# mLSTM: the running sum of the forget gates as a product with a triangle, the sums of the rows one below the other, and gatings first among the streams that are due

## The chip, the cores and the metric

The kernel runs on one core of a Trainium2 chip. A core has a matrix engine (TensorE, PE in the profile; its weight loads are listed apart, as PEld), VectorE (DVE), ScalarE (ACT), GpSimd (POOL) and SyncE (SP), which here only issues DMAs. Each engine works through its own instructions in the order in which the program has them. SBUF is the working memory with 128 partitions; products land in PSUM, which has eight banks of 128 partitions x 512 float32. The metric is the time of one execution on the device, in microseconds; less is better.

## The reference

The input is x of 4 sequences, 512 positions and 256 channels, in float32. Two layers follow. In each, x is normalised, and the outputs of an attention block and of a feed-forward block are added to it.

Layer 0 has an mLSTM block and, beside it, a feed-forward block with eight low-rank experts of which each token uses two. The mLSTM block (8 heads, 16 channels of q and k, 32 of v) computes, for each sequence and head:

```python
logfg = log_sigmoid(f_pre);  Fcum = cumsum(logfg)              # over positions
Dmat  = Fcum[s] - Fcum[t] + i_pre[t],  -inf where t > s
m     = max over t of Dmat;  Smat = exp(Dmat - m)
C     = (q @ k.T / sqrt(dqk)) * Smat
n     = maximum(abs(sum over t of C), exp(-m))
h     = (C / n) @ v
```

followed by a norm of each head, an output gate, w_out, and a gated MLP of 1024 channels (w_gate, w_up, w_down). With g[t] = i_pre[t] - Fcum[t], the row maximum is m[s] = Fcum[s] + max of g[t] over t <= s. So a running sum of logfg and a running maximum of g give all that the exponentials need.

The expert block computes silu(gate) * up for the base and once more for each of two chosen experts, with gate and up shifted by low-rank products. Layer 1 has an attention over the 4 sequences at each position (16 heads) and a feed-forward block of 1024 channels that keeps the two largest of each four.

## The kernel before

Positions are worked off in NJ = 4 tiles j of 128 positions; a tile holds these positions of all B = 4 sequences, so 512 tokens. All products are in float32. TensorE runs a matmul in two passes and a transpose in one, which is why the profile has 3782 of its instructions.

**Order.** The program's order is made by a planner when the kernel is built. Each piece of work is a Python generator, a stream, that yields the time from which it can go on; `Clock` (from line 51) keeps a modelled time for each engine and tile, and `Flow` (from line 223) picks the next stream. `flow.run(main)` steps the main stream whenever it is due and no other stream is; among the other streams `Flow.next` (line 268) takes the one whose time comes first, streams with a flag last. What a stream issues goes into the queues of all engines in that order, so an instruction on VectorE that waits holds up all that the planner put behind it.

In layer 0 the main stream goes through the experts of a tile (`experts`) and then the MLP of the tile before (`mlp`). Beside it run `routing` (low-rank inputs `low`, by way of the transposes `spread`), `following` (norm, transposes and values `vp` of the next tile), and `attention_of_all`, which runs `mlstm(j)` tile by tile. Layer 1 follows with streams of its own.

**Experts.** `order` (line 1106) lists eleven chunks of up to 128 hidden channels x 256 tokens: one "pair" (two halves of 64 rows, packed into the array at once) and ten whole ones. `base(i)` opens a PSUM bank `chunk` and does the base products (chunk<-xnT,wguT: four matmuls, for the pair eight of 64 rows). `gated` (line 1128) reads the bank: a tanh on ScalarE into `sl`, and, as a stream of its own named `rest`, two operations on VectorE, sl<-sl,chunk and the product into `hid` (base) or into `he` (experts; `he_pair` for the pair, `tmp` for the others). Then the low-rank products of the first and of the second expert are added to the same bank (chunk<-low,lora, steps 1 and 2), each only after the gating before it has read the bank. `acc` collects the products from `he`, and at the end those of `hid` with WdT and of `dw` with BdT. A bank that the gatings still read blocks the next step on TensorE. Four banks are opened in advance only while `low` isn't there; after that the loop opens one per round.

**mLSTM.** `mlstm(j)` takes the gate inputs `gz` (tokens on partitions). The log of the forget gate is worked out on VectorE in about 14 small operations (fz, fp, fa) into `lg`, with the input gate beside it. Two transposes `r_ps` bring both to rows: 32 rows (head x sequence) of 128 positions. On VectorE a scan with multiply and add gives the running sum `f_row`, a subtraction `g_row`, a scan with max the running maximum `m_row`, an addition `fm_row`; `m_end` is the last maximum on a diagonal. `carry` hands the last columns to the next tile. `m_row` goes to DRAM and comes back in two DMAs as `ct`, spread over all partitions. Three transposes and a product with `ones` bring g_row, fm_row, m_row and m_end back to columns in the bank `t_ps`; `cols` copies them to SBUF, and `dec` holds the exponents (four sets of 32 columns), which ScalarE exponentiates. GpSimd scales the values with them (`wv`), TensorE makes the new state from that (`kt_ps`, `st_ps`, in the stream `pass_on`).

Then GpSimd masks `ct`, VectorE subtracts g, ScalarE exponentiates, `qk` (packed, 32 rows at a time) is multiplied in, and `by_columns` (line 869) forms hv = ct x va and the row sums: for each half s of the heads, 16 matmuls of 32 output rows x 128 columns into the bank `sums`, with the sequence b as the column block. `to_tokens` (line 876) transposes the two hv and the sums back to tokens (`tok`, four 128x128 transposes each). After that come `den`, `ss` (GpSimd takes its power -1/2), the output gate (`o_ps`), the transposes `pt`, the product `yp` with w_out, which VectorE adds to `xn`, statistics, and the transposes for the MLP.

**Where rows and columns of this meet in the PE array.** A product with fewer than 128 rows or columns of weights is placed in a part of the array: 64 columns for the pair, 32 columns for hv, sums and st_ps, 32 rows for qk, h_ps and t_ps.

Of the kernel before, what the change touches and what calls it, by code (L numbers as in the profile page):

```python
# [28 lines left out]
BANKS = 8  # L29


@with_exitstack
def layers_kernel(ctx: ExitStack, tc: tile.TileContext, io: dict, out: bass.AP):
# [189 lines left out]
    class Flow:  # L223
# [10 lines left out]
        def add(self, gen, wait=0.0, after=False):  # L234

            self.streams.append([self.now + wait, gen, after])
# [150 lines left out]
    ones = new(const, [B * H, P], "ones")  # L387
    nc.gpsimd.memset(ones, 1.0)
    mhalf = new(const, [P, B * H], "mhalf")
# [17 lines left out]
    for base, step in ((0, -2 * DQK), (2 * DQK - 1, 2 * DQK)):  # L407
        nc.gpsimd.affine_select(
            out=own_pair, in_=own_pair, pattern=[[step, H // 2]], compare_op=ALU.is_ge,
            fill=0.0, base=base, channel_multiplier=1 if step < 0 else -1)  # L410
    def inv_sqrt(o, i):
# [60 lines left out]
    with ExitStack() as l0:  # L472
# [22 lines left out]
        pool.memset(ones_at, 0.0)  # L495
# [152 lines left out]
        def mlstm(j):  # L648
# [23 lines left out]
            for s in range(2):  # L672
# [9 lines left out]
            lg = new(sm, [P, 2, H, B], "lg")  # L682
            lf = lg[:, 0, :, :].rearrange("p h b -> p b h")
            dve.tensor_scalar_mul(
                lg[:, 1, :, :].rearrange("p h b -> p b h"), gz[:, :, 0:H], CAP)
# [12 lines left out]
            dve.scalar_tensor_tensor(lf, fp, -2.0, fa, ALU.mult, ALU.add)  # L698
# [15 lines left out]
            yield from flow.wait(lg, banks=1)  # L714

            r_ps = mm_ps("r_ps")
            for n in range(2):
                transpose(  # L720
                    r_ps[0:HB, n * P : (n + 1) * P], lg[:, n, :, :].rearrange("p h b -> p (h b)"),
                    ident)
            yield from flow.wait(r_ps)
            f_row = new(sm, [HB, P], "f_row", 2)
            dve.tensor_tensor_scan(
                f_row, ones[:, 0:1].to_broadcast([HB, P]), r_ps[0:HB, 0:P],
                0.0 if first else carry["F"], ALU.mult, ALU.add)
            g_row = new(sm, [HB, P], "g_row")
            dve.tensor_tensor(g_row, r_ps[0:HB, P : 2 * P], f_row, ALU.subtract)
            m_row = new(sm, [HB, P], "m_row", 2)  # L730
            dve.tensor_tensor_scan(
                m_row, g_row, g_row, LOWEST if first else carry["M"], ALU.max, ALU.max)
            fm_row = new(sm, [HB, P], "fm_row")
            dve.tensor_tensor(fm_row, f_row, m_row, ALU.add)
            carry["F"], carry["M"] = f_row[:, P - 1 : P], m_row[:, P - 1 : P]
# [811 lines left out]
```

## Time and profile before

| | us |
|---|---|
| median of 3 runs | 775.93 (774.78 to 776.19) |
| the profiled execution | 776.43 |
| its span, first to last instruction | 774.6 |
| TensorE busy | 763.0 (99% of the span), 3782 instructions |
| VectorE busy | 471.4 (61%), 1070 |
| ScalarE busy | 225.7 (29%), 457 |
| GpSimd busy | 160.6 (21%), 151 |
| granted TensorE clock, mean | 1.000 |

A line of a group reads: line, engine, operation, out<-in by tile names, rows*columns of the weights, moved size, count | busy time, mean duration in ns | idle time before it. Nearly all lines say L216, the helper that records every operation; the tile names tell them apart. A line of the timeline has start and duration in us; equal instructions that follow each other are merged, with their count. Products overlap, so the time from one start to the next is shorter than a duration. A line of the waits reads: who waits <- who releases it: us in total, times, longest.

Layer 0 ends near 545 us. The four tiles' mLSTM transposes `r_ps` begin at 28.9, 138.5, 253.9 and 387.2 us.

### The profile page before, as it was taken

The page shows a single profiled execution, that of the slowest core. Times are in us where ns is not written, and L with a number is a line of the kernel's source. Part 1 is how long each engine was busy: PE and PEld are TensorE (multiplying, and loading weights), DVE is VectorE, ACT ScalarE, POOL GpSimd, SP SyncE. Part 2 cuts the span into 40 slices and gives each one's busy share as a digit, 9 for nine tenths or more (in the row PEclk, how much of TensorE's full clock was granted, in tenths as well). Part 3 has the DMA queues.
Part 4 walks back from the last instruction along what each step waited for, and adds up shares of the span by engine and source line. Part 5 has one row for each costly group of instructions (what it writes and reads, how often), then busy time and mean ns, then how long its engine had stood idle before and what let it go on. Part 6 is the DMA issues. An engine that isn't in the chain of part 4 may idle for free.

```text
span 774.6 us, 9712 instructions
## 1 busy us (share of the span) xinstructions
PE 763.0 (99%) x3782; PEld 516.6 (67%) x3782; DVE 471.4 (61%) x1070; ACT 225.7 (29%) x457; POOL 160.6 (21%) x151
## 2 busy tenths in 40 slices
PE   6999999999999999999999999999999999999998
PEld 3677786766657776765777774747545575754487
DVE  4878647977552878634378534332366984837980
ACT  2334314332212342313134312010344305243310
POOL 5322051321230410140030041000333203333000
PEclk9999999999999999999999999999999999999999
DMA  8830000300000300000030120001000000000000
GB/s 253 282 97 1 1 1 1 110 1 1 1 1 1 110 0 1 2 0 1 1 110 1 56 96 14 1 0 55 0 1 0 0 28 1 0 28 0 0 28 29
DMA packets 18975, 25.44 MB, mean 33 GB/s; under 512 B 2800, under 2 KB 12784, under 8 KB 18928
## 3 DMA queue, kind: packets, MB, share of 16 engines
q1 hardware_dynamic: 17408, 24.39, 9.9%
q8 instruction: 30, 0.49, 0.3%
q10 hardware_dynamic: 1520, 0.43, 0.2%
q14 instruction: 17, 0.14, 0.1%
HBM read 22.65 MB, written 2.16 MB: 32 GB/s over the span
## 4 chain that ended last, share of the span: by engine, by line
PE 98%; DVE 1%; DMA 1%; ACT 0%; issue 0%
PE chunk L216 20%; PE yp L216 18%; PE up L216 14%; PE gp L216 14%; PE acc L216 11%; PE qk_ps L216 4%; PE vp L216 2%; PE pt L216 2%; PE v_ps L216 2%; PE o_ps L216 2%; PE lp L216 2%; PE qk L216 1%; PE hv L216 1%; PE sums L216 1%; PE k_ps L216 1%; PE q_ps L216 1%
## 5 line engine op out<-in xcount | busy, mean ns | idle before, releaser
L216 ACT ACTIVATE sl<-chunk 128x256 f32<-128x256 f32 x132 | 50.6, 384 | 134.5 <-PE chunk L216 118.1
L216 PE MATMUL chunk<-low,lora 128*128 128x256 f32 (+1 forms) x384 | 87.3, 385 | 0.9 <-DVE he_pair L216 0.7
L216 PE MATMUL chunk<-xnT,wguT 128*128 128x256 f32 (+1 forms) x384 | 84.5, 384 | 0.0
L216 PEld LDWEIGHTS chunk<-xnT,wguT 128*128 128x128 f32 (+1 forms) x384 | 63.6, 181 | 23.5 <-issue 11.5
L216 PEld LDWEIGHTS chunk<-low,lora 128*128 128x128 f32 (+1 forms) x384 | 63.0, 181 | 14.9 <-issue 2.1
L216 DVE SCALAR_TENSOR_TENSOR sl<-sl,chunk 128x256 f32<-128x256 f32 x132 | 54.4, 412 | 11.3 <-ACT sl L216 10.7
L216 PE MATMUL gp<-xnT,wguT 128*128 128x512 f32 x128 | 60.2, 592 | 0.0
L216 PE MATMUL up<-featT,w_up 128*128 128x512 f32 x128 | 60.2, 592 | 0.0
L216 PE MATMUL gp<-featT,w_gate 128*128 128x512 f32 x128 | 60.1, 592 | 0.0
L216 PE MATMUL up<-xnT,lora 128*128 128x512 f32 x128 | 60.1, 592 | 0.0
L216 PE MATMUL yp<-w_down,hid 128*128 128x256 f32 x256 | 56.2, 379 | 0.0
L216 PE MATMUL yp<-w_gate,hs 128*128 128x256 f32 x256 | 56.2, 379 | 0.0
L216 PEld LDWEIGHTS yp<-w_down,hid 128*128 128x128 f32 x256 | 48.5, 190 | 8.2 <-issue 1.7
L216 PEld LDWEIGHTS yp<-w_gate,hs 128*128 128x128 f32 x256 | 48.6, 190 | 6.6
L216 DVE SCALAR_TENSOR_TENSOR tmp<-tmp,gp 128x512 f32<-128x512 f32 x32 | 21.9, 685 | 42.8 <-ACT tmp L216 42.8
L216 ACT ACTIVATE tmp<-gp 128x512 f32<-128x512 f32 x32 | 19.1, 597 | 96.7 <-PE gp L216 96.7
L216 PEld LDWEIGHTS up<-xnT,lora 128*128 128x128 f32 x128 | 24.3, 190 | 29.3 <-issue 28.0
L216 PEld LDWEIGHTS up<-featT,w_up 128*128 128x128 f32 x128 | 24.1, 190 | 27.9 <-issue 26.3
L216 PEld LDWEIGHTS gp<-xnT,wguT 128*128 128x128 f32 x128 | 24.0, 190 | 27.8 <-issue 27.0
L216 PEld LDWEIGHTS gp<-featT,w_gate 128*128 128x128 f32 x128 | 24.1, 190 | 27.6 <-issue 27.3
L216 POOL TENSOR_TENSOR pd<-k,q 128x256 f32<-128x256 f32 (+3 forms) x16 | 25.3, 1583 | 81.8 <-ACT k L216 81.8
L216 PE MATMUL acc<-WdT,hid 128*128 128x256 f32 (+1 forms) x192 | 40.9, 386 | 0.0
(211 smaller groups left out, 1192.0 us busy)
## 6 DMA issues: line engine op xcount, KB each, us to landing
ct<-m_dram SPq DMA_DIRECT2D x8, 1024.0 KB, 8.1
x<-in_x SPq DMA_DIRECT2D x3, 512.0 KB, 9.6
out<-x SPq DMA_DIRECT2D x6, 256.0 KB, 2.1
w_gate<-in_w_gate SPq DMA_DIRECT2D x1, 1024.0 KB, 6.7
w_up<-in_w_up SPq DMA_DIRECT2D x1, 1024.0 KB, 7.6
w_down<-in_w_down SPq DMA_DIRECT2D x1, 1024.0 KB, 10.6
wguT<-in_f_gate SPq DMA_DIRECT2D x1, 1024.0 KB, 5.0
lora<-in_f_up SPq DMA_DIRECT2D x1, 1024.0 KB, 5.0
```

The source lines that it names most:

```text
L216: return tc.keep_in_program_order(f(*args, **kw))
```

## The change

Five things change, all in layer 0 (the flags are renamed in layer 1 as well).

1. The running sum of the forget gates is no scan: f_ps = triangle x log_f on TensorE, with the new constant `up_to` (ones where the column isn't before the row), while positions are still on partitions. VectorE takes g and f from it into the two halves of `by_pos`, and one 128x128 transpose `r_ps` makes rows of both. The sum starts at zero in each tile; `m_end`, `f_end` and `ends` carry the offset from tile to tile.
2. One scan is left, a max of r_ps with the constant `lowest`, into rows 0 to 31 of `by_row`, which is zero elsewhere. One 128x128 transpose and one product with 64 columns (`at_end`: the last maximum on a diagonal, and log_f, whose column sums are the last running sums) make `t_ps`. `cols` is gone: the operations that made `dec` read `t_ps` in PSUM.
3. The sums of the four sequences go to the same 128 columns of `sums`, in rows 2b + s of each block of 32, so the matmuls of all b accumulate; the copy shrinks to 128 columns and the third `tok` to one transpose.
4. `add(..., after=True)` becomes `turn=1`, and the stream `rest` of `gated` gets `turn=-1`: it goes ahead of every other stream that is due.
5. Where the last opened chunk's base gating isn't done by the planner's clock and a bank is free, the loop in `experts` opens further bases, up to AHEAD = 4 in advance.

On GpSimd the constants and zeroed tiles add a memset of `lowest`, the selection for `up_to` and three memsets to the set-up ahead of the first norm.

```diff
+AHEAD = 4
...
-        def add(self, gen, wait=0.0, after=False):
+        def add(self, gen, wait=0.0, turn=0):
-            self.streams.append([self.now + wait, gen, after])
+            self.streams.append([self.now + wait, gen, turn])
...
-    ones = new(const, [B * H, P], "ones")
+    ones = new(const, [P, P], "ones")
+    lowest = new(const, [B * H, 1], "lowest")
+    nc.gpsimd.memset(lowest, LOWEST)
+    up_to = new(const, [P, P], "up_to")
+    nc.gpsimd.affine_select(
+        out=up_to, in_=ones, pattern=[[1, P]], compare_op=ALU.is_ge, fill=0.0, base=0,
+        channel_multiplier=-1)
...
+        by_pos = new(sm, [P, P], "by_pos")
+        by_row = new(sm, [P, P], "by_row")
+        at_end = new(sm, [P, 2 * HB], "at_end")
+        for t in (ones_at, by_pos, by_row, at_end):
+            pool.memset(t, 0.0)
+        g_col, f_col, log_f = (t.rearrange("p (h b) -> p h b", b=B) for t in (
+            by_pos[:, 0:HB], by_pos[:, HB : 2 * HB], at_end[:, HB:]))
...
-            lg = new(sm, [P, 2, H, B], "lg")
-            dve.tensor_scalar_mul(
-                lg[:, 1, :, :].rearrange("p h b -> p b h"), gz[:, :, 0:H], CAP)
...
+            f_ps = mm_ps("f_ps")
+            mm(f_ps[:, 0:HB], up_to, at_end[:, HB:], start=True, stop=True)
+            f_hb = f_ps[:, 0:HB].rearrange("p (h b) -> p h b", b=B)
+            dve.scalar_tensor_tensor(
+                g_col, gz[:, :, 0:H].rearrange("p b h -> p h b"), CAP, f_hb, ALU.mult,
+                ALU.subtract)
+            dve.tensor_copy(f_col, f_hb)
+            yield from flow.wait(by_pos, banks=1)
             r_ps = mm_ps("r_ps")
-            for n in range(2):
-                transpose(r_ps[0:HB, n * P : (n + 1) * P], lg[:, n, :, :]..., ident)
+            transpose(r_ps[:, 0:P], by_pos, ident)
             yield from flow.wait(r_ps)
-            dve.tensor_tensor_scan(f_row, ones[:, 0:1]..., r_ps[0:HB, 0:P], ..., ALU.mult, ALU.add)
-            dve.tensor_tensor(g_row, r_ps[0:HB, P : 2 * P], f_row, ALU.subtract)
-            dve.tensor_tensor_scan(m_row, g_row, g_row, ..., ALU.max, ALU.max)
-            dve.tensor_tensor(fm_row, f_row, m_row, ALU.add)
+            m_row = by_row[0:HB, :]
+            dve.tensor_tensor_scan(
+                m_row, lowest.to_broadcast([HB, P]), r_ps[0:HB, 0:P],
+                LOWEST if first else carry["M"], ALU.max, ALU.max)
             if not last:
-                dve.tensor_scalar_mul(m_end, ident[0:HB, 0:HB], carry["M"])
+                dve.tensor_scalar_mul(
+                    at_end[0:HB, 0:HB], ident[0:HB, 0:HB], m_row[:, P - 1 : P])
+                dve.tensor_copy(f_end, r_ps[HB : 2 * HB, P - 1 : P])
+                dve.tensor_tensor(m_end, f_end, m_row[:, P - 1 : P], ALU.add)
+                carry["M"] = m_end
...
-            for n, row in enumerate((g_row, fm_row, m_row)):
-                transpose(t_ps[:, n * HB : (n + 1) * HB], row, ident[0:HB, 0:HB])
+            transpose(t_ps[:, 0:P], by_row, ident)
             if not last:
-                mm(t_ps[:, 3 * HB : 4 * HB], ones, m_end, start=True, stop=True)
+                mm(t_ps[:, P : P + 2 * HB], ones, at_end, start=True, stop=True)
             yield from flow.wait(t_ps)
-            dve.tensor_copy(cols..., t_ps...)
-            dve.tensor_scalar_mul(dec[:, 0, :, :], cols[:, 1, :, :], -1.0)
+            m_col = t_ps[:, 0:HB].rearrange("p (h b) -> p h b", b=B)
+            dve.scalar_tensor_tensor(dec[:, 0, :, :], m_col, -1.0, f_col, ALU.mult, ALU.subtract)
...
+                dve.tensor_copy(ends[:, 0, :, :], m_all)
+                dve.tensor_tensor(ends[:, 1, :, :], f_all, m_all, ALU.add)
...
-                        mm(out[32 * r : 32 * r + 32, cols_of(b)], lhsT(b, r),
-                           ct[s][:, r, cols_of(b)], start=start and b == 0, stop=stop, ...)
+                        o = out[32 * r : 32 * r + 32, :]
+                        mm(o if n_of(o) == P else o[:, cols_of(b)], lhsT(b, r),
+                           ct[s][:, r, cols_of(b)], start=start and b == 0, stop=..., ...)
...
-                for b in range(B):
+                for b in range(B if n < 2 else 1):
                     transpose(tok[:, cols_of(b)], hvT[n][:, cols_of(b)], ident)
...
-                by_columns(sums, lambda b, r: ones_at[:, b, DV - s : 2 * DV - s], s, s == 0, s == 1)
+                by_columns(
+                    sums[:, 0:P], lambda b, r: ones_at[:, b, DV - 2 * b - s : 2 * DV - 2 * b - s], s,
+                    s == 0, s == 1)
-                    act.copy(hvT[2], sums)
+                    act.copy(hvT[2], sums[:, 0:P])
...
-                flow.add(rest())
+                flow.add(rest(), turn=-1)
...
-                if i == len(order) - 1:
+                while (0 < i and len(rooms) < min(i + AHEAD, len(order)) and clock.room(1) <= flow.now
+                       and (read[i - 1] < 0 or clock.over(rooms[i - 1]) > flow.now)):
+                    yield from base(len(rooms))
+                if len(rooms) == len(order):
                     based.add(j)
```

## The prediction

> **What bounds the kernel now.** First the page: busy times and the chain that ended last.
>
> ```profile
> PE 763.0 (99%) x3782; PEld 516.6 (67%) x3782; DVE 471.4 (61%) x1070; ACT 225.7 (29%) x457; POOL 160.6 (21%) x151
> ...
> PE 98%; DVE 1%; DMA 1%; ACT 0%; issue 0%
> ```
>
> TensorE is the chain. VectorE's 61% hides beside it, so an edit counts by the TensorE time it adds or removes and by the places where TensorE comes to stand. Where it stands today is in the waits of TensorE:
>
> ```profile
> PE pt L216 <- DVE xn L216: 5.9, 2, 5.7
> PE vp L216 <- ACT xnT L216: 1.4, 1, 1.4
> PE chunk L216 <- DVE he_pair L216: 0.7, 1, 0.7
> ...
> PE chunk L216 <- DVE tmp L216: 0.2, 1, 0.2
> ```
>
> The first two are the start of the kernel, which the change leaves alone. In the whole middle only two places are left to win. The timeline of the first shows also how I count:
>
> ```profile
> 115.74 1.03 PE L216 MATMUL yp<-w_out,featT 128*128 128x256 f32 x4
> 116.60 1.03 PE L216 MATMUL chunk<-low,lora 128*128 128x256 f32 x4
> ...
> 116.80 0.69 DVE L216 TENSOR_TENSOR xn<-yp,xn 128x512 f32<-128x512 f32 x1 [1.03 <-PE yp L216]
> 117.41 0.41 DVE L216 SCALAR_TENSOR_TENSOR sl<-sl,chunk 128x256 f32<-128x256 f32 x1
> ...
> 117.85 0.42 DVE L216 TENSOR_TENSOR he_pair<-chunk,sl 128x256 f32<-128x256 f32 x1
> ...
> 118.33 0.44 PE L216 MATMUL chunk<-low,lora 128*64 128x256 f32 x2 [0.71 <-DVE he_pair L216]
> ```
>
> Durations overlap, so I price TensorE from start to start. Four passes of 256 columns take 116.60 - 115.74 = 0.86 us, 0.216 each (a matmul is two passes, a transpose one). The next four should end at 117.46; TensorE goes on at 118.33. Of that 0.87, 0.09 is a change of array shape (below) and 0.78 is a stall: the gating of the pair stood in VectorE's queue behind xn<-yp, which itself waited for the second yp. The other one, at 122.44 behind a tmp gating, is 0.39 by the same count.
>
> The groups by form give the small products that the change rewrites (mean durations, not intervals):
>
> ```profile
> L216 PE MATMUL tok<-ident,ct 128*128 128x128 f32 x48 | 6.2, 275 | 0.0
> ...
> L216 PE MATMUL r_ps<-ident,lg 128*32 128x128 f32 x8 | 1.5, 272 | 0.0
> L216 PE MATMUL t_ps<-m_end,ones 32*128 32x32 f32 x6 | 1.1, 271 | 0.0
> ```
>
> and the timeline around t_ps of the last tile gives the price of a change of array shape:
>
> ```profile
> 388.56 1.99 PE L216 MATMUL chunk<-xnT,wguT 128*128 128x256 f32 x8
> 390.49 0.24 PE L216 MATMUL t_ps<-ident,g_row 32*128 32x32 f32 x1
> 390.57 0.22 PE L216 MATMUL t_ps<-ident,fm_row 32*128 32x32 f32 x1
> 390.63 0.22 PE L216 MATMUL t_ps<-ident,m_row 32*128 32x32 f32 x1
> 390.79 0.48 PE L216 MATMUL chunk<-low,lora 128*128 128x256 f32 x1
> ```
>
> Eight passes of 0.216 are 1.73; they take 1.93. 0.10 of it is paid after the 64-column group ahead of them and 0.094 on leaving for the 32-row array. So an excursion costs 0.094 on leaving, about as much at its end, and 0.104 on the first wide product after it. Single intervals bear this out: 310 ns instead of 216 before a small array, 320 after one. r_ps is an exception; around it the intervals stay at 216 and 110.
>
> **What the change removes from TensorE**, four tiles together. The two r_ps transposes per tile: 8 x 0.109 (28.92 to 29.14 is two) = 0.87. The t_ps groups: 33.04 to 33.56 is 0.52, the same in the next two tiles, 0.30 in the last, 1.86 in all; leaving for them 4 x 0.094 = 0.38; the wide product after them 3 x 0.104 = 0.31. The third tok goes from four transposes to one: 12 x 0.109 = 1.31. Sum 4.73.
>
> **What it adds.** f_ps, 8 passes of 32 columns on the full array; t_ps from the zero-padded at_end, 6 passes of 64 columns; r_ps and t_ps, one full transpose per tile each, 8 x 0.109 = 0.87. No row has a short pass on the full array. Bounds: 0.061 (the 32-column transposes above) and 0.216 (a 256-column pass). I take 0.11: t_ps<-m_end does 32 columns in 0.112 and a full transpose, which also loads 128 columns of weights, 0.109. 14 x 0.11 = 1.54 (0.85 to 3.02). Added 2.41; net -2.3. The sums products don't shrink: 128 of 32x128 stand in both programs; only their addresses change.
>
> **The order.** Counting array shapes along both programs (r_ps left out): 82 changes before, 74 after, which is the t_ps excursions alone; wide products that follow a small array 36 and 29, three of those already counted, so -4 x 0.104; 128-column ones 3 and 6 at 0.056 (tok's first interval is 165 to 169). That is -0.25. TensorE's work: -2.55.
>
> **Stalls that go.** With gatings ahead of other due work, he_pair stands before both xn<-yp, and up to four bases are issued before the first low product. Both stalls go: -1.17. What is late next there is low itself: the spread transpose moves behind ten more WdT products, and POOL's two low (2.5 us) wait behind the 5.5 us pow of ss. Counted from o_ps's end: five WdT products (2.2) and BdT (0.9) come before x<-acc (0.7), which holds VectorE to 3.9; the reduction of ss (1.2) and three small operations bring 5.8, the pow 11.3, low 13.9. TensorE needs low at 16.1: ten more WdT products and spread to 7.9, BdT 0.9, the pair 2.2, three chunks 5.2. That is 2.2 us to spare.
>
> **Stalls that come.** In the first tile the pair's second low step needs he_pair from its first:
>
> ```profile
> 30.96 2.15 PE L216 MATMUL chunk<-low,lora 128*64 128x256 f32 x12
> ...
> 32.09 0.38 ACT L216 ACTIVATE sl<-chunk 128x256 f32<-128x256 f32 x1 [0.64 <-DVE sl L216]
> ...
> 32.51 0.42 DVE L216 SCALAR_TENSOR_TENSOR sl<-sl,chunk 128x256 f32<-128x256 f32 x1
> 32.96 0.42 DVE L216 TENSOR_TENSOR he_pair<-chunk,sl 128x256 f32<-128x256 f32 x1
> ```
>
> The pair ends at 31.97, he_pair at 33.38: 1.4 us, just covered by a low step and t_ps (33.56). After the change the fourth base, too, comes before r_ps, and VectorE's queue reads: gating of that base, scan, at_end, f_end, m_end, then he_pair. By the rows, from the end of spread at 23.5: the pair 1.9, three bases of 1.73 and f_ps bring 30.9; tanh and gating of the last base end at 32.4, the scan (0.41) and the three small ones (0.5) at 33.35, he_pair at 34.2. TensorE, after r_ps, the pair's first step, the next chunk's and t_ps, arrives at 33.45: 0.75 us late. In the last tile the same distance shrinks to a low step and one transpose (1.0 us), with a base's gating and the scan ahead of he_pair: 0.65. Together +1.4; bounds 0 (TensorE itself arrives that much later) and 1.6 (two of the old 0.78). Places reckoned to be tight but not late (r_ps behind the new f_ps in tiles 1 and 2; hv of tile 1) get +0.2, between 0 and 1.0.
>
> **At no cost**, with the cover named. VectorE's edits: a scan (0.41 to 0.47), g_row 0.28, fm_row 0.28 and cols 0.28 go, six or seven of 0.15 to 0.22 come; cover is TensorE's own work between t_ps and st_ps, 6.9 us of which dec, exp and POOL's wv use 4.2. POOL's five new set-up instructions (0.1 to 0.3 each, 0.9 together) fall in its idle 1.64 us before the first rstd at 4.29; beyond that each microsecond would push the start. The second round trip (f_ps, by_pos, r_ps) brings m_row, its three SP DMAs and POOL's selections some 2 us later; the ct of the first tile is selected at 43.9 and first subtracted at 49.9, and the last subtraction is at 73.3. Nothing else waits in SP's queue then. The new wait itself, VectorE's by_pos for f_ps, holds up the gating of the next base behind it, which TensorE needs only two steps on; behind r_ps, which waits for by_pos, stand a low step or a base, and that is the tight place priced above. The copy of sums on ScalarE shrinks from 0.59.
>
> [...]
>
> The copy that is dropped, cols, took 278 ns with four readers of 180 after it, 1.0 us per middle tile. Now four operations read t_ps in PSUM (206 each, as the third tok's reader does) and two don't: 1.18, under the cover above.
>
> **The sum**: -2.55 - 1.17 + 1.4 + 0.2 = -2.1 us. It is made against the profiled execution, 776.43 us (span 774.6 and 1.8 around it), 0.5 above the median of 775.93; I take it off the median: 773.8.
>
> **Rivals.** (a) The new stalls don't form, since VectorE has room: -2.55 - 1.17 = -3.7, 772.2. For it: TensorE is busy through the whole middle today though many distances are as tight. Against: the queue order just read. (b) The order eats the gain: passes at 0.216 (+1.5), or the tight places late, end near -0.6, 775.3. For it: one more round trip in each tile. (c) Slower: low of the second tile comes late. The price is one for one beyond the 2.2 us to spare, so from 5.8 us later than reckoned the kernel is over 0.2% slower (+1.55; 777.5). For it: POOL's pow holds low already and two x<-acc are moved ahead of VectorE's work on ss and low. Against: 5.8 us is a whole further pow.
>
> **Chances.** About 0.2% (1.55 us) is what a measurement can tell from no change. My forecast 0.53, (a) 0.18, (b) 0.21, (c) 0.08. Faster begins below 774.4, 0.6 above the forecast: (a) and 0.46 of the forecast, 0.64. Same: the other 0.07 and (b), 0.28. Slower: 0.08. All bounds at their best give 771.5, at their worst 776.3; the range from 772.2, where (a) lies, to 775.8, past (b), leaves out the outer part of (a) and (c), under 2 in 10.
>
> **What would show it.** t_ps, r_ps and f_ps with no interval over 0.22 beside them; tok at 36; waits of TensorE for he_pair near 33 and near 391 in place of 118, 0.6 to 0.8 each; no wait for low near 115. Wrong if TensorE waits elsewhere for more than 1 us, or if short passes on the full array cost over 0.15.

## The result

The changed kernel takes 774.59 us, the median of 21 executions (773.97 to 775.33). The kernel before, measured beside it on the same chip, takes 775.70 (774.63 to 776.33, 21 executions). The ratio is 0.9987 with a 95% interval of 0.9981 to 0.9993: faster by 1.1 us. That is real, but within the 0.2% that I had called no change, and to which the prediction gave a chance of 0.28. The forecast was 773.8, a gain of 2.1 against the 775.93 that was then known; 774.59 is inside the range of 772.2 to 775.8. Half of the gain is missing, and the question is where it went.

The page of the changed kernel, busy times and the chain that ended last:

```profile
PE 761.0 (98%) x3766; PEld 516.1 (67%) x3766; DVE 470.9 (61%) x1070; ACT 224.6 (29%) x457; POOL 162.5 (21%) x156
...
PE 91%; DVE 6%; DMA 1%; ACT 1%; issue 0%; POOL 0%; DVEq 0%; POOLq 0%
```

TensorE has 16 instructions fewer, as the edits have it. The chain says more: before, 98% of it lay on TensorE and 1% on VectorE, now 91% and 6%. VectorE is no busier than it was. It is late at more places.

The profiled execution took 775.33 us (span 773.6). The profiles differ in the start: the first expert product begins between 21.7 and 23.5 us in the profiles of this study. Layer 1 takes 230.15 us in all of them but one (231.8 with the planner's other cost). So I compare the stretch of layer 0, from the first chunk<-xnT to the first qk_ps. The timeline of TensorE after the change has its ends:

```profile
23.23 1.08 PE L217 MATMUL chunk<-xnT,wguT 128*64 128x256 f32 x8
...
543.43 1.88 PE L217 MATMUL qk_ps<-WdT,xnT 128*128 128x512 f32 x4
```

543.43 - 23.23 = 520.20 us, and 544.48 - 23.48 = 521.00 before: **-0.8 us**. (The other 0.3 of the 1.1 lies in the start, which spreads by more than that.)

The waits of TensorE in the changed kernel (who waits <- who releases it: us in total, times, longest):

```profile
PE pt L217 <- DVE xn L217: 6.2, 3, 5.6
PE vp L217 <- ACT xnT L217: 1.4, 1, 1.4
PE chunk L217 <- DVE he_pair L217: 1.1, 2, 0.9
PE chunk L217 <- DVE hid L217: 0.4, 1, 0.4
PE yp L217 <- ACT oT L217: 0.2, 1, 0.2
```

he_pair is there twice, as forecast. But there is a third wait for xn, in the middle of the kernel, and one for a hid gating. The prediction named neither. By intervals from start to start, as in the prediction, the places are:

| us | TensorE waits for | lost | forecast |
|---|---|---|---|
| 33 | he_pair of the first tile | 0.94 | 0.75 |
| 390.5 | he_pair of the last tile | 0.31 | 0.65 |
| 160.9 | hid gating in the second tile, with 0.10 on the product after it | 0.67 | part of +0.2 |
| 187.1 | spread of the routing, with 0.06 after it | 0.29 | part of +0.2 |
| 275.6 | xn of the norm in the third tile, with 0.06 after it | 0.88 | part of +0.2 |

Together 3.09, where 1.27 went (0.78, 0.39 and 0.10 on the product after the second). With TensorE's work, counted below as -2.6, this closes: -2.6 + 3.09 - 1.27 = -0.8.

**160.9.** The timeline there (start and duration in us):

```profile
155.49 3.06 DVE L217 TENSOR_SCALAR xn<-x,mv,rstd 128x256 f32<-128x256 f32 x4
156.40 4.01 POOL L217 TENSOR_SCALAR_AFFINE_SELECT ct<-ct 128x2048 f32<-128x2048 f32 x2
...
159.18 1.51 DVE L217 TENSOR_TENSOR dw<-tmp 128x256 f32<-128x256 f32 x1
...
160.04 1.09 PE L217 MATMUL pt<-ident,xn 128*128 128x128 f32 x8
...
161.05 0.42 DVE L217 TENSOR_TENSOR hid<-chunk,sl 128x256 f32<-128x256 f32 x1
...
161.53 1.13 PE L217 MATMUL chunk<-low,lora 128*128 128x256 f32 x4 [0.40 <-DVE hid L217]
```

dw, an addition of two tiles in SBUF, takes 1.51 us here; it takes 0.42 in six of the seven other places (0.78 in one). It ends 0.28 after GpSimd's second selection of ct (160.41). The fourth xn is held in the same way by the first selection: four take 3.06 us, of which the fourth 2.10, where an undisturbed one takes 0.40. The gating of hid stands behind dw in VectorE's queue, and TensorE behind that gating.

**187.1.** Here GpSimd is the one that is late. Its copy tmp<-rank, from which `spread` is made, began 0.22 us after a subtraction of VectorE on ct with two inputs in SBUF:

```profile
185.83 1.22 DVE L217 TENSOR_TENSOR ct<-ct,by_pos 128x1024 f32<-128x1024 f32 x1
...
186.05 1.47 POOL L217 COPY tmp<-rank 128x512 f32<-128x512 f32 x1 [22.49 <-DVE rank L217]
...
187.57 0.66 PE L217 MATMUL spread<-ident,tmp 128*128 128x128 f32 x4
```

The copy took 1.47 us; in the other three tiles it takes 0.61 to 0.65. With 0.65 it would have ended at 186.70, before TensorE came to spread (187.35). In all seven profiles of this study in which the copy begins under such a subtraction it takes 1.47, in all other places at most 0.69. No run takes this overlap alone away, so this stall is read from the traces and not tested.

**275.6.** Here the small rstd is held (1.32 us; 0.16 before the change) by a selection, and then three of the four xn (0.72 each) by GpSimd's products hr:

```profile
268.17 2.01 POOL L217 TENSOR_SCALAR_AFFINE_SELECT ct<-ct 128x2048 f32<-128x2048 f32 x1 [1.37 <-DMA ct<-m_dram]
...
268.88 1.32 DVE L217 TENSOR_SCALAR rstd<-mv 128x4 f32<-128x4 f32 x1
...
274.21 2.33 DVE L217 TENSOR_SCALAR xn<-x,mv,rstd 128x256 f32<-128x256 f32 x4
274.42 2.61 POOL L217 TENSOR_TENSOR hr<-hr,dec 128x264 f32<-128x264 f32 x4
...
276.60 0.76 PE L217 MATMUL pt<-ident,xn 128*128 128x128 f32 x5 [0.32 <-DVE xn L217]
```

These rows together: dw took 1.51 us instead of 0.42 and rstd 1.32 instead of 0.16, and each ends just behind a selection of GpSimd (0.28 and 0.02 us after it); the other way round GpSimd's copy took 1.47 instead of 0.61 and ends 0.47 after the subtraction. What makes one engine wait for the other no run here shows.

### The profile page after: what moved, and what is told of

The parts are those of the page before. It is cut to its first block, busy times and chain, and to the rows that moved or that the text cites. A ratio compares the mean times of both kernels' runs of the same rounds, so it can differ in the third digit from the quotient of the medians.

```text
span 773.6 us, 9684 instructions
## 1 busy us (share of the span) xinstructions
PE 761.0 (98%) x3766; PEld 516.1 (67%) x3766; DVE 470.9 (61%) x1070; ACT 224.6 (29%) x457; POOL 162.5 (21%) x156
## 4 chain that ended last, share of the span: by engine, by line
PE 91%; DVE 6%; DMA 1%; ACT 1%; issue 0%; POOL 0%; DVEq 0%; POOLq 0%
PE yp L217 18%; PE chunk L217 16%; PE up L217 14%; PE gp L217 14%; PE acc L217 10%; PE qk_ps L217 4%; PE vp L217 2%; PE pt L217 2%; PE o_ps L217 2%; PE v_ps L217 2%; PE lp L217 2%; DVE sl L217 1%; PE qk L217 1%; PE hv L217 1%; PE q_ps L217 1%; DVE tmp L217 1%
## 5 line engine op out<-in xcount | busy, mean ns | idle before, releaser
L217 PE MATMUL acc<-tmp,lora 128*128 128x512 f32 x80 | 40.8, 598 | 0.0
```

The lines of the kernel that those rows point to most:

```text
L217: return tc.keep_in_program_order(f(*args, **kw))
```

## The experiments

Theory A: TensorE's work shrank as priced, and the missing microsecond is VectorE held by GpSimd. Theory B: the stalls come from gatings that are now ahead of the norm and the routing. All times below are medians beside the kernel before on the same chip; "layer 0" is the stretch defined above (before 521.0, after 520.2).

| run | us | ratio to before, 95% | layer 0 |
|---|---|---|---|
| after | 774.59 | 0.9987 (0.9981 to 0.9993) | 520.2 |
| order alone (parts 4, 5) | 773.78 | 0.9979 (0.9970 to 0.9988) | 519.7 |
| products alone (parts 1 to 3) | 775.49 | 0.9998 (0.9990 to 1.0007) | 521.1 |
| after without selections in tiles 2, 3 | 773.11 | 0.9966 (0.9953 to 0.9978) | 518.7 |
| after, f_ps of 128 columns | 774.57 | 0.9987 (0.9979 to 0.9996) | 520.2 |
| order and sums (parts 3, 4, 5) | 773.33 | 0.9970 (0.9960 to 0.9980) | 518.4 |
| after, m_end later | 774.10 | 0.9985 (0.9976 to 0.9994) | 520.0 |
| after, selections split | 773.87 | 0.9978 (0.9969 to 0.9988) | 519.4 |
| after, planner told the hold | 781.88 | 1.0082 (1.0057 to 1.0107) | 524.1 |
| order, sums, rows stacked | 775.04 | 1.0000 (0.9990 to 1.0010) | 522.5 |
| gatings ahead alone (part 4) | 774.12 | 0.9978 (0.9969 to 0.9987) | 519.5 |
| the stacked one, selections split | 773.30 | 0.9972 (0.9959 to 0.9984) | 519.8 |
| gatings ahead and sums (parts 3, 4) | 773.06 | 0.9964 (0.9951 to 0.9976) | 518.3 |

### The parts apart

The order on the kernel before:

```diff
-                flow.add(rest())
+                flow.add(rest(), turn=-1)
...
-                if i == len(order) - 1:
+                while (0 < i and len(rooms) < min(i + AHEAD, len(order)) and clock.room(1) <= flow.now
+                       and (read[i - 1] < 0 or clock.over(rooms[i - 1]) > flow.now)):
+                    yield from base(len(rooms))
+                if len(rooms) == len(order):
                     based.add(j)
```

> The kernel before with parts 4 and 5 of the change alone (gatings ahead, up to four bases opened ahead); products and sums as before. TensorE's work by the counts of this program: 3 fewer changes of array (3 x 0.094), 4 fewer wide products after a small array (4 x 0.104), one narrow one more (0.056): -0.64 us. Theory A (the missing microsecond is VectorE held up while GpSimd selects ct, and ct comes later because of the second round trip): the order by itself wins the stalls near 118 and 122 (-1.2), keeps one at he_pair in the first tile (+0.8), and makes none above 0.5 us near 150 to 165 or 265 to 280: -0.6 -1.2 +0.8 = -1.0, about 774.7. Rival B (gatings ahead of the norm's and routing's instructions make the new stalls): TensorE waits for xn or for a gating of hid behind the norm in the second and third tile here too, about 1.5 us together: +0.5, about 776.2.

Measured 773.78, layer 0 down 1.3: more than the whole change wins. In the middle of the kernel the only wait of TensorE that the trace names is 0.2 for he_pair, where I had expected 0.8; xn and hid are waited for nowhere. Theory B falls: the order by itself makes none of the new stalls.

The products without the order, that is the changed kernel with the lines above taken back:

> The kernel after without parts 4 and 5 (gatings take their turn, no bases ahead): triangle product, single transposes and sums one below the other remain. TensorE's work by the counts of this program, with the excursions at their measured 0.22: -2.1 us. Theory A: the two old stalls stay (1.2), a collision of VectorE with GpSimd's selections of ct costs 0.5 to 1.5 somewhere in the middle tiles: between -1.6 and -0.6, about 774.6. Rival B (the stalls come from the order): no new stall above 0.3, the whole -2.1 shows: 773.6, a microsecond better than the change as a whole.

Measured 775.49, no gain at all, though 2.1 us of TensorE's work are gone. Theory B is out here too. The stall near 118 is gone here too; of the two old ones only that behind a tmp gating is left (0.38 at 120). The stalls that eat the gain are not the collision that I expected, but the new round trip itself:

```profile
PE r_ps L217 <- DVE by_pos L217: 1.0, 2, 0.5
PE chunk L217 <- DVE hid L217: 0.8, 2, 0.4
PE chunk L217 <- DVE he_pair L217: 0.6, 1, 0.6
```

In the third and the last tile r_ps stands directly behind f_ps on TensorE, which waits 0.65 for by_pos and then 0.49 for a gating that stood behind by_pos on VectorE: 1.14 in each, and 0.63 at he_pair in the first tile. In the whole change the bases opened ahead stand between f_ps and r_ps, and this does not occur.

### GpSimd's selections

Four instructions left out, the order of all others unchanged (`unsent` has the planner count the selection, and nothing is issued):

```diff
-                pool.affine_select(
+                sel = (pool if j not in (1, 2) else unsent)
+                sel.affine_select(
...
-                    act.activation(c, c, AF.Exp, scale=-1.0)
+                    act.activation(c, c, AF.Exp, scale=-1.0 if j not in (1, 2) else 0.0)
```

> The kernel after without GpSimd's four selections of ct in the second and third tile; every other instruction stands in the same order. What is left out is the masking of later positions in these tiles (and the exponent there is scaled by zero, so that the values stay finite). Theory A: VectorE's dw of the second tile falls from 1.5 to 0.42 us and its rstd of the third from 1.3 to 0.16; the stalls of TensorE at 160.9 (0.67 with the slower product after it) and at 275.6 (0.88) go: -1.5, about 773.1. Rival B (VectorE is late because gatings stand ahead of the norm): the stall at 275.6 stays above 0.6, and at most 0.7 is won. Either way the stalls at 33 (0.94) and 390.5 (0.31) stay.

Measured 773.11; layer 0 is 1.54 shorter than the changed kernel's, against 1.55 expected from the table of stalls. The waits of TensorE, and the line of dw (shortest, median and longest in ns), first of this run, then dw of the changed kernel:

```profile
PE pt L217 <- DVE xn L217: 5.8, 2, 5.6
PE vp L217 <- ACT xnT L217: 1.3, 1, 1.3
PE chunk L217 <- DVE he_pair L217: 1.1, 2, 0.9
PE yp L217 <- ACT oT L217: 0.2, 1, 0.2
```

```profile
L217 DVE TENSOR_TENSOR dw<-tmp x8: 424/426/780, 67.0 to 441.8; 128x256 f32<-128x256 f32 x8
```

```profile
L217 DVE TENSOR_TENSOR dw<-tmp x8: 424/425/1506, 67.7 to 444.0; 128x256 f32<-128x256 f32 x8
```

The wait for hid and the third wait for xn are gone; he_pair stays, and so does the stall at spread. So the two stalls at 160.9 and 275.6 come from these selections. That is shown: every engine's instructions stand in the same order without them. At 160.9 the way is plain, dw held; it takes 0.74 here (under GpSimd's products hr) and not the 0.42 expected, which is enough. At 275.6 the selections act in two ways that this run doesn't separate: the first holds rstd, and the second brings GpSimd's products hr onto xn. Without the selections hr begins at 269.95, and xn, at 271.93, meets only the last of it.

A second test of the same: each selection as two over half the heads, all else in the same order.

```diff
-                pool.affine_select(
-                    out=ct[s], in_=ct[s], pattern=[[0, H // 2 * B], [1, P]],
-                    compare_op=ALU.is_ge, fill=FAR, base=0, channel_multiplier=-1)
+                clock.issue("pool", "affine_select", (), {"out": ct[s], "in_": ct[s]})
+                for r in range(0, H // 2, 2):
+                    piece = ct[s][:, r : r + 2, :]
+                    tc.keep_in_program_order(nc.gpsimd.affine_select(
+                        out=piece, in_=piece, pattern=[[0, 2 * B], [1, P]],
+                        compare_op=ALU.is_ge, fill=FAR, base=0, channel_multiplier=-1))
```

> The kernel after, with each of GpSimd's selections of ct (2.01 us) as two over half the heads; every other instruction stands in the same order. If VectorE gets its turn between two selections, dw of the second tile starts at 159.4 instead of 160.4 and the stall at 160.9 (0.67 with the slower product behind it) goes; in the third tile rstd comes a microsecond earlier, but GpSimd's power for it still stands behind the selection, so the stall at 275.6 falls only by 0.3: -1.0 in all, about 773.6. If VectorE waits until GpSimd's whole run of selections is over, dw stays at 1.5 us and nothing is won: 774.6.

Measured 773.87. The interval overlaps the changed kernel's, so the reading rests on the profile, where layer 0 is shorter by 0.8. VectorE gets its turn between two selections:

```profile
154.79 2.15 DVE L217 TENSOR_SCALAR xn<-x,mv,rstd 128x256 f32<-128x256 f32 x4
155.71 4.46 POOL L861 TENSOR_SCALAR_AFFINE_SELECT ct<-ct 128x1024 f32<-128x1024 f32 x4
...
157.58 0.59 DVE L217 TENSOR_TENSOR dw<-tmp 128x256 f32<-128x256 f32 x1
```

dw takes 0.59 instead of 1.51, and the stall at 160.9 is gone (-0.67); at 275.6 0.71 of 0.88 is left. There rstd takes only 0.33, but the next small operation of the norm is held by the second half (0.79 instead of 0.16).

Then the planner. Its cost of such an operation on VectorE adds the hold, but no more than the operation's own duration once again. Told the whole of it:

```diff
-                us += max(0.0, min(us, self.free["pool"] - start))
+                us += max(0.0, self.free["pool"] - start)
```

> The kernel after, with one term of the planner's costs changed: an operation of VectorE that reads two tiles of SBUF while GpSimd works is charged the whole rest of GpSimd's work; so far it is charged at most its own duration once more. The plan moves: by its counts TensorE's work is 0.2 us more than after's. If the stalls of the second and third tile come from VectorE's operations being held longer than the planner knew, the new plan goes round them: -1.5 +0.2, about 773.3. If a plan that knows this puts other work late instead, stalls of about 2 us remain at other places and the time stays within 0.5 of 774.6.

Measured 781.88, worse than both kernels. The four executions took 779.31 and 779.97 at a mean granted clock of 1.000 and 0.999, and 783.78 and 783.99 at 0.996; what follows is read from the first. The stalls at 160.9 and 275.6 are gone, or nearly: of the second 0.4 stays. But the new plan puts four of the norm's statistics with their aggregates and two small operations ahead of a gating at 126, and TensorE waits 2.3 us there, 1.2 and 1.0 around f_ps at 257, 0.4 before he_pair at 31 and 0.5 behind kt_ps at 270. A truer cost for one term didn't make a better plan. Why it chose this order I haven't taken apart.

### he_pair

Two small operations on VectorE moved behind the wait for t_ps:

```diff
             if not last:
                 dve.tensor_scalar_mul(
                     at_end[0:HB, 0:HB], ident[0:HB, 0:HB], m_row[:, P - 1 : P])
-                f_end = new(sm, [HB, 1], "f_end")
-                dve.tensor_copy(f_end, r_ps[HB : 2 * HB, P - 1 : P])
-                m_end = new(sm, [HB, 1], "m_end", 2)
-                dve.tensor_tensor(m_end, f_end, m_row[:, P - 1 : P], ALU.add)
-                carry["M"] = m_end
...
             yield from flow.wait(t_ps)
+            if not last:
+                f_end = new(sm, [HB, 1], "f_end")
...
```

> The kernel after, with f_end and m_end (two operations of VectorE of 0.15 us) issued after the wait for t_ps and not before it; TensorE's order is the same. By my reading he_pair of the first tile stands behind the scan, at_end, f_end and m_end: without the last two it comes 0.34 us earlier, and the stall at 33 falls from 0.94 to 0.6: -0.3, about 774.3. If the stall is set by something else (the gating's tanh, the bank), it stays at 0.94.

Measured 774.10, by its interval not to be told from the changed kernel; the reading rests on the profile. (VectorE and ScalarE also take a few other instructions in another order there, between 61 and 82 us, behind the stall at 33.) This is the place in the changed kernel:

```profile
32.02 0.40 DVE L217 TENSOR_TENSOR_SCAN by_row<-lowest,r_ps 32x128 f32<-32x128 f32 x1
...
32.46 0.23 DVE L217 TENSOR_SCALAR at_end<-ident,by_row 32x32 f32<-32x32 f32 x1
32.72 0.15 DVE L217 COPY f_end<-r_ps 32x1 f32<-32x1 f32 x1
...
32.91 0.15 DVE L217 TENSOR_TENSOR m_end<-f_end,by_row 32x1 f32<-32x1 f32 x1
...
33.54 0.42 DVE L217 TENSOR_TENSOR he_pair<-chunk,sl 128x256 f32<-128x256 f32 x1
...
34.11 0.44 PE L217 MATMUL chunk<-low,lora 128*64 128x256 f32 x2 [0.87 <-DVE he_pair L217]
```

Between m_end and he_pair stands the gating's first operation, sl<-sl,chunk (33.08, 0.42 us). The queue is the one that the prediction read off. With f_end and m_end out of it the stall is 0.45 instead of 0.94, somewhat better than the 0.6 expected. But layer 0 gained only 0.2: TensorE arrives earlier everywhere behind, and at 160.9, where dw is held until GpSimd is through, it now waits 0.82 instead of 0.56. What was won ahead of that stall, which hangs on another engine, was partly given back there.

### Short passes

f_ps with 128 columns in place of 32, all else in the same order:

```diff
-        at_end = new(sm, [P, 2 * HB], "at_end")
+        at_end = new(sm, [P, HB + P], "at_end")
...
-            mm(f_ps[:, 0:HB], up_to, at_end[:, HB:], start=True, stop=True)
+            mm(f_ps[:, 0:P], up_to, at_end[:, HB:], start=True, stop=True)
```

> The kernel after with 128 columns instead of 32 in the f_ps product (the other 96 are zeros or unused); every other instruction stands in the same order. A pass of 32 columns starts the next instruction after 0.028 us, but the second of a pair takes 0.112 and the first wide pass after it 0.083 more, 0.223 in all. If a short pass only exposes the load of the next weights, 128 columns cost 2 x 0.109 = 0.218 and the wide pass after them nothing: no change, 774.6, and the interval after f_ps falls from 299 to 216 ns. If columns are what is paid, on top of the 0.083: 4 x (0.218 + 0.083 - 0.223) = +0.3, and the 299 ns stay.

Measured 774.57, layer 0 the same to 0.02 us. TensorE's timeline of the changed kernel, and then with 128 columns:

```profile
386.39 0.30 PE L217 MATMUL f_ps<-at_end,up_to 128*128 128x32 f32 x2
386.53 1.97 PE L217 MATMUL chunk<-xnT,wguT 128*128 128x256 f32 x8
388.34 0.27 PE L217 MATMUL r_ps<-ident,by_pos 128*128 128x128 f32 x1
```

```profile
386.26 0.38 PE L217 MATMUL f_ps<-at_end,up_to 128*128 128x128 f32 x2
386.48 1.89 PE L217 MATMUL chunk<-xnT,wguT 128*128 128x256 f32 x8
388.21 0.27 PE L217 MATMUL r_ps<-ident,by_pos 128*128 128x128 f32 x1
```

From the first f_ps to r_ps it is 1.95 both times. With 32 columns f_ps itself is over in 0.14, but the eight passes behind it take 1.81; with 128 columns it takes 0.22, and they 1.73, which is eight times 0.216. That is the first of the two readings: no change. Whether it is the load of the weights that a short pass exposes, this run doesn't separate.

### What the triangle is worth

The order with the sums one below the other, without the triangle and its transposes:

```diff
-                        mm(out[32 * r : 32 * r + 32, cols_of(b)], lhsT(b, r),
+                        o = out[32 * r : 32 * r + 32, :]
+                        mm(o if n_of(o) == P else o[:, cols_of(b)], lhsT(b, r),
...
-                for b in range(B):
+                for b in range(B if n < 2 else 1):
                     transpose(tok[:, cols_of(b)], hvT[n][:, cols_of(b)], ident)
```

> The kernel before with parts 3, 4 and 5 (sums one below the other, gatings ahead, bases ahead), without the triangle product and the single transposes of parts 1 and 2. Theory A' (the second round trip of the triangle makes every new stall, the order and the sums make none): the order by itself gave 773.78, twelve transposes of 0.109 fewer give 1.31 more: 772.5, two microseconds below the change as a whole. Rival (the stalls come when any product gets shorter, because the plan is shifted): stalls of 1 us or more between 30 and 400 in this profile, 773.5 or more.

Measured 773.33. Layer 0 is 1.3 shorter than with the order alone (518.4 against 519.7), which is the twelve transposes at 0.109. So parts 1 and 2 cost: with them TensorE has 0.6 less work, and the stretch is 1.8 longer. The time expected was 772.5; in two of the eight executions 0.7 to 1.1 us more than the usual 1.8 lie around the span, and I don't know why.

To see which half of parts 1 and 2 does it, g, f+m and m stacked in one zeroed tile, with the scans and r_ps of before, and one full transpose:

```diff
-            fm_row = new(sm, [HB, P], "fm_row")
-            dve.tensor_tensor(fm_row, f_row, m_row, ALU.add)
+            dve.tensor_tensor(rows[HB : 2 * HB, :], f_row, m_row, ALU.add)
+            act.copy(rows[2 * HB : 3 * HB, :], m_row)
...
-            for n, row in enumerate((g_row, fm_row, m_row)):
-                transpose(t_ps[:, n * HB : (n + 1) * HB], row, ident[0:HB, 0:HB])
+            transpose(t_ps[:, 0:P], rows, ident)
             if not last:
-                mm(t_ps[:, 3 * HB : 4 * HB], ones, m_end, start=True, stop=True)
+                mm(t_ps[:, 3 * HB : 4 * HB], ones, at_end, start=True, stop=True)
```

> Parts 3, 4 and 5 as in the order-and-sums kernel, and of part 2 only the single full transpose for t_ps with the zero-padded product: the scans, r_ps and the copy to cols stay as before, so there is no second round trip. g, f+m and m stand below each other in one zeroed tile of 128 rows (one copy of m on ScalarE more). By the counts of this program TensorE's work is 2.9 us below before, 0.95 below the order-and-sums kernel. If it was the round trip of f_ps and by_pos that made the stalls, none comes here: 0.95 below the 773.33 of the order-and-sums kernel, 772.4, and the stretch from the first expert product to the first product of layer 1 falls from 518.4 to 517.5. If the full transpose with its product itself brings VectorE late (he_pair at 33), 0.5 to 0.9 of it is lost again.

Measured 775.04, and a stretch of 522.5 in the profile. The profiled execution, 777.77, is one of four of the twelve that are some 3 us longer, and about 1.7 us of its stretch is a fallen clock (last section); without that it is 520.8, still 2.4 above the order-and-sums kernel. My theory in the form "the second round trip makes the stalls" falls: there is none here, and he_pair is late all the same (0.50 at 33, 0.53 at 260, 0.65 at 393), by my reading since the t_ps that covered it is shorter (not tested). And VectorE is held, in the second tile, worse than ever:

```profile
153.82 4.16 DVE L217 TENSOR_SCALAR xn<-x,mv,rstd 128x256 f32<-128x256 f32 x4
153.90 2.01 POOL L217 TENSOR_SCALAR_AFFINE_SELECT ct<-ct 128x2048 f32<-128x2048 f32 x1
...
155.87 2.60 POOL L217 TENSOR_TENSOR hr<-hr,dec 128x264 f32<-128x264 f32 x4
```

The four xn take 4.16 us. The first takes 2.23: its record begins 0.08 before that of GpSimd's selection and ends 0.15 after it. The other three, 0.72 each, met the products hr. The same with split selections (the edit shown above):

> The stacked kernel with each selection of ct as two over half the heads, every other instruction in the same order. There the four operations xn of the second tile took 4.2 us (the first 2.23, held by a selection, the others 0.72 each, held by the products of hr), TensorE waited 1.6 us for them at 156 to 158, and in the profile its clock then fell to half for 3.5 us. If the hold ends with the selection that runs, the first xn ends a microsecond earlier, the wait falls to about 0.6, the clock stays up: 775.0 - 1.0 = 774.0 by the median, and no execution near 777.7. If the hold lasts while any of GpSimd's work is queued, the wait stays at 1.6 and some executions stay at 777.7.

Measured 773.30. The longest execution is 775.45, none near 777.7. The first xn now takes 0.40, as it should; but the second and third take 1.18 and 1.17, and the four 3.24. By the gaps between records, the yardstick of that 1.6, TensorE waits 1.0 us, not 0.6; from start to start it is 1.4 against 2.3, so 0.9 of the expected 1.0 came. Layer 0, 519.8, is 1.0 below the 520.8. Here the smaller pieces on GpSimd made two shorter holds out of a long one.

Last, the gatings alone, without the bases ahead, and that with the sums; both are made of lines shown above.

> The kernel before with part 4 alone: gatings ahead of the other streams that are due, no bases opened ahead. By its counts TensorE's work is 0.59 us less than before's. If the gatings' place is what takes away the stalls at 118 and 122, the stretch from the first expert product to layer 1 falls from 521.0 by 0.6 + 1.2 to about 519.3, as in the run of parts 4 and 5 together (519.7), and the time to about 774. If the bases ahead are what covers he_pair there, the stall near 118 stays and 1.0 of the gain is missing: 775.0.

> The kernel before with parts 3 and 4 only (sums one below the other, gatings ahead; no bases opened ahead). The gatings alone brought the stretch from the first expert product to layer 1 to 519.5, the twelve transposes are 1.31 less: 518.2, the same as with the bases ahead (518.4), about 773.0. If the shorter sums shift the plan so that something new is late, the stretch stays above 519 and the bases ahead were needed.

774.12 (layer 0 519.5) and 773.06 (518.3). So part 5 brings nothing beside part 4. In the whole change its bases stand between f_ps and r_ps; parts 1 to 4 without it were not run. Parts 3 and 4 are the shortest version: 0.9964 (five executions) against 0.9987 of the changed one, with intervals that don't meet. Its waits of TensorE are those of the start and of layer 1, and nothing else:

```profile
PE pt L216 <- DVE xn L216: 5.7, 1, 5.7
PE vp L216 <- ACT xnT L216: 1.2, 1, 1.2
PE yp L216 <- ACT oT L216: 0.2, 1, 0.2
PE pt L216 <- DMA wk<-in_wk: 0.2, 1, 0.2
```

## Why the prediction was right, and where it failed

- **TensorE's work, -2.55: right.** In the trace the t_ps groups are 1.86 less, leaving for them 0.37, the third tok 1.31, the passes after a small array 0.56; f_ps costs 4 x 0.223 = 0.89, the product for t_ps 0.62, and the two full transposes as much as the old r_ps. That is -2.6. The single term with no row, 14 short passes at 0.11 = 1.54, measures 1.51, though not as I thought: the first pass of a pair takes 0.028 (32 columns) or 0.058 (64), the second 0.112, and the wide pass after it 0.083 or 0.056 more. So "no interval over 0.22 beside f_ps" was wrong (0.299), and the sum right.
- **Stalls that go, -1.17: right**, with 0.10 on the product after the second.
- **he_pair in the first and the last tile, +1.4: right in kind and nearly in sum** (0.94 + 0.31 = 1.25). Each of the two is off, 0.94 for 0.75 and 0.31 for 0.65, and that they offset each other is luck; the run with m_end later shows the queue that was read.
- **low of the second tile, 2.2 us to spare: right that there is no wait, the room too large.** low ends at 112.00 and its first product begins at 112.90, so 0.9 was left. Rival (c) didn't come.
- **PSUM reads: a little too dear.** The prediction took 0.206 us for each of the four operations that read t_ps in PSUM. They take 0.176 to 0.191; dec<-t_ps takes 0.18, as dec<-cols took from SBUF.
- **"Other tight places", +0.2 with bounds 0 to 1.0: this is the step that failed.** They measure 0.67 + 0.29 + 0.88 = 1.84, outside the bounds. None of them is at the places that I named: r_ps behind f_ps and hv of the second tile cost nothing in the whole change. By the prediction's own sign (TensorE waits elsewhere for more than 1 us) it is wrong here in the sum, though no single wait is that long. That the time lies in the range all the same is owed to the range's width.
- The cause is a line under **"At no cost"**. I wrote that m_row and "POOL's selections" come some 2 us later, and looked only at who needs ct (6 us of room). I did not ask whom GpSimd's selections hold up while they run. In the second tile r_ps begins at 144.3 and no longer at 138.5, the selections moved from 152.1 to 156.4 (and in the third tile from 264.3 to 268.2, so some 4 us and not 2), and dw from 163.5 to 159.2: they met. (The 0.29 at spread is, by the trace, the same the other way round: GpSimd held by VectorE.) The profile of before had shown what that costs. It has an rr of 128x4 that takes 1.98 us under the second selection, where 0.16 is usual; the prediction doesn't mention it:

```profile
152.07 3.97 POOL L216 TENSOR_SCALAR_AFFINE_SELECT ct<-ct 128x2048 f32<-128x2048 f32 x2
...
154.08 1.98 DVE L216 TENSOR_SCALAR rr<-rr 128x4 f32<-128x4 f32 x1
```

- **Rival (b)**, the order eats the gain through the round trip, is what the products show when they stand alone: no gain. In the whole change another thing eats it. **Rival (a)**, no new stalls, didn't come for the change; the kernel with parts 3 and 4 has none.
- What stays open: the 0.29 at spread (187.1) is read from the traces and not tested. And why the selections come so late in the middle tiles is not taken apart: with parts 1 to 3 alone they begin at 148.8 and 262.6, earlier than before the change, and hold neither dw nor rstd, so the order of parts 4 and 5 has a share in it.

## What to carry to other kernels

When a change moves work of GpSimd by some microseconds, ask not only who waits for its result but which operations of VectorE run at the same time: here dw, with two SBUF inputs, took 1.51 us for 0.42 under a selection, and two plain tensor_scalar operations 1.32 for 0.16 (rstd) and 2.10 for 0.40 (xn), and the gating of hid, which stood behind dw in VectorE's queue, was late too. It can go the other way as well: GpSimd's copy of the routing took 1.47 us for 0.61 behind a subtraction of VectorE. When TensorE is the bound and a producer is just covered, a shorter product ahead of the wait can give its gain back (by my reading, not tested, in the stacked kernel, where he_pair is late by 0.50, 0.53 and 0.65 us): price an edit by the stretch up to the next wait, not by its own instructions. And take a change apart before judging it: here two of five parts made all of the gain, and two others took more than half of it away again.

## What the runs showed of the hardware that I had not expected

- **The short pass of f_ps cost as much as one of 128 columns.** With 32 columns through the full array and with 128 this matmul of two passes took the same 0.22 us, if the passes after it are counted (1.95 us from f_ps to r_ps both times). The 96 columns more were free there.
- **After the stalls seen here the next pass is slower**, not only after a small array: 0.10 on a 256-column pass (161.53, 320 ns instead of 216), 0.06 on a 128-column one.
- **The clock fell at a place where TensorE's longest gap between records was 0.74 us.** The windows of the stacked kernel, profiled at 777.77 us (start and end, length, busy us and instructions of TensorE, its weight loads, VectorE, ScalarE and GpSimd; then TensorE's granted clock, the DMA share and its GB/s):

```profile
154.00:156.00 2.00, 1.46 (x5) 0.30 (x4) 2.00 (x2) 0.00 (x0) 2.00 (x2) 1.00 0.00 0
156.00:158.00 2.00, 0.96 (x3) 0.41 (x3) 2.00 (x5) 0.00 (x0) 2.00 (x4) 1.00 0.00 0
158.00:160.00 2.00, 1.97 (x8) 1.79 (x9) 1.93 (x8) 1.17 (x2) 1.06 (x2) 0.52 0.00 0
160.00:162.00 2.00, 2.00 (x7) 1.68 (x6) 1.28 (x6) 0.00 (x0) 0.00 (x0) 0.62 0.00 0
```

TensorE waited for xn four times (0.74, 0.25, 0.31 and 0.32 us by the gaps between records, 1.6 together; 2.3 from start to start) and was busy for 2.42 of the 4 us from 154 to 158, and from 158.0 on its passes took twice as long: the clock was 0.52 and 0.62, and passes of 256 columns took 0.427 instead of 0.216 until 161.3. That is about 1.7 us on top of the stall in this profile. Four of the twelve executions are like it (776.7 to 777.8, mean granted clock 0.998; the other eight 774.4 to 775.4 at 1.000). In the profiled execution with the planner's other cost a single wait of 2.3 us left the next passes at full speed (four of 256 columns in 0.97 us, which is four times 0.216 and 0.10); in two of the other three executions of that kernel the mean granted clock was 0.996, and they took about 4 us longer, at a place of which there is no trace. What decides it I can't tell from these runs.
